# Casting, summing and testing the adjacency in half-row pieces during the graph convolutions of a four-layer graph network

## The chip, the cores and the metric

The kernel runs on one core of one Trainium2 chip. The metric is the device time of one execution in microseconds (us). A core has five engines that run side by side and meet at semaphores: TensorE (PE), VectorE (DVE), ScalarE (ACT), GpSimd (POOL) and SyncE (SP), which here only issues DMAs. Each engine runs its own list of instructions in order.

## What is computed

Sixteen graphs of N = 1024 nodes with D = 128 features; `adj` is a matrix of zeros and ones, 1024 x 1024 fp32 for each graph. Four residual layers follow each other, each on a layer norm with ReLU of x:

```python
def reference(x, adj, nodemask, ...):
    h = relu(layernorm(x)); x = x + gnn(h, adj, nodemask)     # dilate adj, three SAGE convolutions with batch norm, then Wl
    h = relu(layernorm(x)); x = x + attention(h, adj)         # softmax(q k' * scale + log(max(adj, 1e-8))), 4 heads
    h = relu(layernorm(x)); x = x + gat(h, adj)               # softmax over leaky_relu(s_i + s_j) where adj > 0
    h = relu(layernorm(x)); x = x + gcn(h, adj)               # D^-1/2 (adj + 1) D^-1/2 h W' + b, D from the row sums of adj + 1
    return x
```

The dilation drops neighbours row by row, and only the first layer uses its result. The other three layers use the whole `adj`. The batch norm of a convolution takes its mean and variance over all graphs, so each convolution layer ends before the next begins.

## The kernel before

The kernel has three stages, one after the other: `dilate_plain` (to about 690 us), `convolutions_plain` (to about 1606 us) and `attentions_plain` (to the end), and a short `verdict`. The fast path assumes, among other things, that `adj` holds only zeros and ones, is symmetric and has no empty row. Tests of this write into the tile `trouble` and the row sums into `deg`; `verdict` reads both at the end, and a general path runs if they speak against it.

**Dilation** leaves the thinned matrices of all graphs in a DRAM tensor `kept` as fp8 and reciprocal row sums in `rdeg`.

**Convolutions.** `neighbours(b, h)` (from line 1020) loads the thinned matrix of graph b (tile `C`, 1 MB, two buffers) and the reciprocal degrees broadcast to all partitions (`rdb`, 512 KB, two buffers), both on SP's queue. PE transposes h (L1029), ACT copies it out (L1030); a `Splitter` makes three bf16 parts of h on ACT and DVE (L676 to L679); PE multiplies them with C (L1040, 48 matmuls of 512 columns for a graph), and DVE scales the sums by `rdb` (L1042). A first loop over the graphs normalises x (loaded by POOL's queue, two buffers) and calls `neighbours`. Then three layers loop over the graphs: PE makes the output o (L1087 to L1094), ACT squares it (L1099), DVE sums the squares (L1100), POOL takes the power of -1/2 (`rsqrt`, L1045), ACT applies scale and ReLU (L1106), and in the first two layers `neighbours` follows. ACT's queue stores the result in `spill` (L1116). PSUM holds the outputs of two graphs, two neighbour sums and two turns. In this stage the framework orders the instructions of each engine when the program is built, by program order as priority and by its own estimate of when each is ready; the chip then keeps that order.

**Attention.** Seven generators (`matrices`, `before`, `attend`, `values`, `positive`, `gat`, `gcn`) each walk through the graphs. Each step says, with `yield`, which engine it needs next, for how long and from when; `in_order` (a planner that runs when the program is built) takes the step that can start first, on a tie one that is not for PE, and then the generator that lags most, and so fixes the order of each engine by hand. SP's DMAs stand in the order in which the generators emit them.

- `matrices` (L1301 to L1333) admits graph b once attention is done for the graphs up to b - 2 and the last layer up to b - 4 (`done["attend"] < b - 1`, `done["gcn"] < b - 3`). For each of eight row blocks it loads 128 x 1024 of `adj` in fp32 (L1309, 512 KB, two buffers `a`); ACT casts it to fp8 into the tile `A` with a ReLU and sums the rows (L1310); DVE tests for values other than zero and one (L1314); PE subtracts the turned blocks from the blocks below the diagonal (L1321, L1323) and ACT sums the absolute differences (L1327), which is the test of symmetry. `dinv` is made from `deg` (L1330, L1332). `A` has four buffers.
- `before` loads x and the three spilled convolution outputs (`h_a`, `hT_a`) on SP's queue, applies the layer's last product (L1354, L1357), the norm (L1274), turns it (L1283) and makes q, k and v (L1375, L1295).
- `attend` writes 16 A into PSUM (ACT, L1408), adds q k' (PE, L1413) and takes exponentials (ACT, L1421); `values` multiplies them with v and with ones (PE, L1444) and divides (DVE, L1450, L1452).
- `positive`, `gat` and `gcn` are the other two layers: masks (DVE, L1495), products with them (PE, L1555, L1570, L1624) and their sums (L1558, L1573), on splits into bf16 parts (L1541 to L1547, L1607 to L1613).

Of the kernel before, what the change touches and what calls it, by code (L numbers as in the profile page):

```python
# [6 lines left out]
F32 = mybir.dt.float32  # L7
# [5 lines left out]
ALU = mybir.AluOpType  # L13
# [948 lines left out]
def convolutions_plain(tc, x, ident, ap, xp, h0, minus_half, kept, rdeg, spill, final, Wr, Wx, bias, gamma, beta, Wl, bl):  # L962
    nc = tc.nc
    with ExitStack() as ctx:
# [3 lines left out]
        w2 = ctx.enter_context(tc.tile_pool(name="c_work", bufs=2))  # L968
        pso = ctx.enter_context(tc.tile_pool(name="c_out", bufs=4, space=PSUM))
# [76 lines left out]

        for b in range(B):
# [27 lines left out]
        wr_s, wx_s, constant = wr[0], wx[0], row_parts(b6[0], "const0")  # L1075
        for l in range(3):
            stats = kp.tile([P, 2 * B, 6], F32, name="stats")
            for b in range(B):
                if l:
                    rd6 = xp.tile([6, N], F32, name="xt")  # L1080
                    nc.sync.dma_start(rd6, rdeg[b][None, :].to_broadcast([6, N]))
                    has = w2.tile([6, N], BF16, name="has")
# [20 lines left out]
                rsqrt(nrm[:, 1, :], nrm[:, 0, :])  # L1103
                h = w2.tile([P, NB, D], F32, name="h")
# [3 lines left out]
                if l < 2:  # L1108
                    neighbours(b, h)
                else:  # L1110
# [38 lines left out]
        nc.vector.tensor_copy(final[3][0:3], row_parts(last, "const3")[0:3])  # L1149

# [55 lines left out]
def attentions_plain(tc, x, spill, final, ready_weights, adj, deg, trouble, eye, out, scores, bound, reach):  # L1206
    nc = tc.nc
    with ExitStack() as ctx:
# [7 lines left out]
        lp = ctx.enter_context(tc.tile_pool(name="f_load", bufs=2))  # L1216
# [28 lines left out]
        nc.vector.memset(trouble, 0.0)  # L1245
# [54 lines left out]
        def matrices():  # L1300

            for b in range(B):
                while done["gcn"] < b - 3 or done["attend"] < b - 1:
                    yield
                m = adp.tile([P, NB, N], F8, name="A")
                for i in range(NB):
                    t = yield "ACT", 1.3, 0.0, 0
                    a = lp.tile([P, N], F32, name="a")
                    nc.sync.dma_start(a, adj[b, i * P:(i + 1) * P, :])  # L1309
                    nc.scalar.activation(m[:, i, :], a, AF.Relu, accum_out=deg[:, b, i:i + 1], saturate=False)  # L1310
                    yield "DVE", 1.4, 0.0, 0
                    junk = lp.tile([P, N], F8, name="junk", bufs=1)

                    nc.vector.scalar_tensor_tensor(junk, a, 0.0, a, op0=ALU.is_gt, op1=ALU.not_equal,  # L1314
                                                   accum_out=trouble[:, b, i, 0:1], saturate=False)
                    for hf in range(2):
                        w = min(HN, (i - 4 * hf) * P)
                        if w > 0:
# [8 lines left out]
                            nc.scalar.activation(junk[:, :w], ps[:, :w], AF.Abs, accum_out=trouble[:, b, i, 1 + hf:2 + hf])  # L1327
# [412 lines left out]
def whole(tc, x, adj, nodemask, chunk_mats, chunk_mask, eye, sel, p, out):  # L1740
    nc = tc.nc
    with tc.tile_pool(name="dram", bufs=1, space=DRAM) as dp, tc.tile_pool(name="keep", bufs=1) as kp:
# [19 lines left out]
        with tc.tile_pool(name="final", bufs=1) as fp:  # L1762
            final = [fp.tile([P, D], F32, name=f"final{i}") for i in range(3)] + [fp.tile([3, D], BF16, name="final_row")]
            with tc.tile_pool(name="early", bufs=1) as yp, tc.tile_pool(name="c_adj", bufs=2) as ap, \
                    tc.tile_pool(name="c_x", bufs=2) as xp:
                ident = yp.tile([P, P], F32, name="ident")
                nc.sync.dma_start(ident, eye)
                minus_half = yp.tile([P, NB], F32, name="minus_half")
# [4 lines left out]
                convolutions_plain(tc, x, ident, ap, xp, h0, minus_half, kept, rdeg, spill, final, *layer0)  # L1773
            attentions_plain(tc, x, spill, final, ready_weights, adj, deg, trouble, eye, out, scores, bound, reach)
# [45 lines left out]
```

## Time and profile before

| | |
|---|---|
| median of 3 runs | 4039.99 us (4030.87 to 4042.07) |
| the profiled execution | 4039.04 us, span of its trace 4037.3 us |
| mean granted PE clock | 0.926 of full speed |
| PE busy | 3474.4 us (86%), 26756 matmuls |
| DVE busy | 2527.9 us (63%) |
| ACT busy | 2401.7 us (59%) |
| POOL busy | 794.7 us (20%) |
| read from and written to DRAM | 287.98 MB and 51.19 MB |

Busy time is summed over the span, so it mixes stages with different limits; the stages have to be looked at one by one. Instructions that only issue a DMA are not counted as busy, though they take time on their queue (SP, ACT or POOL). A line such as "PE x L1 <- ACT y L2: 10, 5, 3" in the table of waits means that PE's instructions of line 1 came late by 10 us in total, 5 times, at most 3 us, and that an instruction of line 2 on ACT ended the wait.

### The profile page before, as it was taken

To read this page: it belongs to the slowest core of one execution; us is meant where nothing else is said; L and a number is where in the kernel's file an instruction comes from. 1 tells how busy PE (TensorE), PEld (TensorE's weight loads), DVE (VectorE), ACT (ScalarE), POOL (GpSimd) and SP (SyncE) were. 2 spreads that over 40 slices of the span, in tenths; PEclk is the share of its full clock that TensorE was granted. 3 is DMA by queue.
4 is the path that set the end of the run, shared out by engine and by line. 5 is a ranking of instruction groups with operands and counts; after the bars stand their busy time and mean duration, and the time that the engine had idled before them with its cause. 6 is when DMAs were issued, how large, how long until landed. Compare 5 with 4: busy or idle time off the path is not lost.

```text
span 4037.3 us, 65855 instructions
## 1 busy us (share of the span) xinstructions
PE 3474.4 (86%) x26756; PEld 1998.6 (50%) x26756; DVE 2527.9 (63%) x4782; ACT 2401.7 (59%) x3961; POOL 794.7 (20%) x680
## 2 busy tenths in 40 slices
PE   4888887999999987778989988998898989989775
PEld 2556565445555566324444444444454444454333
DVE  4988774543344343328776876776777686777656
ACT  3778764543333334676667776767666767766540
POOL 7545521210000011101111112112111101211110
PEclk9999887999999998799999998999998999999887
DMA  9632223443333312411221221122122022111000
GB/s 106 40 21 16 14 97 116 165 159 126 125 111 121 108 68 85 142 37 53 74 79 43 64 79 60 51 74 74 43 69 80 26 74 79 58 59 48 27 17 17
DMA packets 182500, 293.21 MB, mean 73 GB/s; under 512 B 77468, under 2 KB 124456, under 8 KB 173992
## 3 DMA queue, kind: packets, MB, share of 16 engines
q1 hardware_dynamic: 91944, 221.69, 16.8%
q0 software_dynamic: 79728, 24.66, 7.5%
q10 hardware_dynamic: 10512, 42.54, 2.6%
q8 instruction: 212, 3.47, 0.4%
q14 instruction: 104, 0.85, 0.1%
HBM read 287.98 MB, written 51.19 MB: 84 GB/s over the span
## 4 chain that ended last, share of the span: by engine, by line
PE 58%; DVE 15%; ACT 7%; DMA 3%; issue 2%; POOL 2%; ACTq 0%; SPq 0%; POOLq 0%; DVEq 0%
PE g L1040 12%; PE acc L1444 9%; PE sum L1570 9%; PE t L1413 5%; PE sum L1624 4%; PE sum L1555 4%; DVE pm L1495 3%; PE o L1093 2%; PE sum L1357 2%; PE o L1094 2%; PE sum L1375 1%; ACT e L1421 1%; DVE rden L1450 1%; PE t L1029 1%; PE sum L1295 1%
## 5 line engine op out<-in xcount | busy, mean ns | idle before, releaser
L1421 ACT ACTIVATE e<-t 128x1024 f32<-128x1024 f32 x512 | 508.2, 1023 | 489.3 <-PE t L1413 472.9
L1495 DVE SCALAR_TENSOR_TENSOR pm<-dst,minus,A 128x1024 fp8e4<-128x1024 f32 x512 | 676.2, 1350 | 7.9 <-DMA dst<-scores 7.9
L1040 PE MATMUL g<-C,parts 128*128 128x512 fp8e4 x2304 | 521.3, 381 | 15.4 <-DVE aggT L1042 9.2
L1408 ACT ACTIVATE t<-A 128x2048 f32<-128x2048 fp8e4 x256 | 482.3, 1884 | 3.9 <-ACT dst L1475 0.3
L1570 PEld LDWEIGHTS <-pm 128*128 128x128 fp8e4 x4096 | 347.0, 98 | 187.1 <-issue 165.3
L1570 PE MATMUL sum<-parts,pm 128*128 128x198 bf16 x4096 | 400.3, 251 | 26.0 <-DVE pm L1495 16.3
L1444 PE MATMUL acc<-e,va 128*32 128x512 f32 x2048 | 330.5, 616 | 41.3 <-ACT e L1421 38.4
L1040 PEld LDWEIGHTS <-parts 128*128 128x128 bf16 x2304 | 223.1, 98 | 262.7 <-ACT parts L678 5.7
L1413 PE MATMUL t<-qT,kT 32*128 32x512 f32 x2048 | 307.7, 672 | 31.7 <-ACT t L1408 31.3
L1444 PE MATMUL acc<-e,ones_hd 128*32 128x512 f32 x2048 | 319.7, 601 | 0.0
L1573 DVE TENSOR_REDUCE pos<-sum 128x132 f32<-128x396 f32 x256 | 145.0, 566 | 204.0 <-PE sum L1570 203.4
L1555 PE MATMUL sum<-parts,A 128*128 128x396 bf16 x1024 | 210.8, 351 | 44.2 <-DVE parts L1547 23.9
L1042 DVE TENSOR_TENSOR aggT<-g,rdb 128x512 f32<-128x512 f32 x96 | 66.2, 690 | 269.2 <-PE g L1040 269.1
L1045 POOL TENSOR_TENSOR nrm<-nrm,minus_half 128x8 f32<-128x8 f32 x48 | 79.6, 1662 | 639.8 <-DVE nrm L1102 639.8
L1624 PE MATMUL sum<-A,gparts 128*128 128x512 fp8e4 x768 | 178.0, 385 | 24.9 <-ACT gparts L1607 17.6
L835 DVE TENSOR_TENSOR r<-ya,both 128x512 bf16<-128x512 f16 x184 | 140.2, 776 | 92.7 <-ACT ya L832 91.9
L1099 ACT ACTIVATE sq<-o 128x512 f32<-128x512 f32 x96 | 55.8, 599 | 226.1 <-PE o L1094 224.3
L1267 POOL TENSOR_TENSOR ln_st<-ln_st,minus_half 128x8 f32<-128x8 f32 x48 | 86.1, 1794 | 511.8 <-DVE ln_st L1265 377.1
L882 DVE SCALAR_TENSOR_TENSOR rows<-y,thirty,rows 128x1024 fp8e4<-128x1024 f16 x128 | 169.9, 1335 | 25.4 <-ACT y L874 24.6
L1555 PEld LDWEIGHTS <-A 128*128 128x128 fp8e4 x1024 | 94.5, 99 | 182.0 <-issue 104.1
L1106 ACT ACTIVATE h<-o,nrm 128x128 f32<-128x128 f32 x384 | 105.7, 384 | 116.9 <-POOL nrm L1045 113.7
L885 POOL TENSOR_TENSOR own<-rows,lower 128x256 bf16<-128x256 fp8e4 x128 | 109.5, 866 | 330.6 <-DVE rows L882 197.2
(287 smaller groups left out, 6937.7 us busy)
## 6 DMA issues: line engine op xcount, KB each, us to landing
a<-in_adj_dram SPq DMA_DIRECT2D x128, 512.0 KB
C<-kept SPq DMA_DIRECT2D x48, 1024.0 KB
dst<-scores SPq DMA_DIRECT2D x64, 512.0 KB
rdb<-rdeg SPq DMA_DIRECT2D x48, 512.0 KB
spill<-hT ACTq DMA_DIRECT2D x48, 512.0 KB
kept<-rows ACTq DMA_DIRECT2D x16, 1024.0 KB
h_a<-spill SPq DMA_DIRECT2D x64, 256.0 KB
hT_a<-spill SPq DMA_DIRECT2D x16, 512.0 KB
```

Source lines behind the costliest of these rows:

```text
L835: nc.vector.tensor_tensor(r, ya, both[:, 1, :, None].to_broadcast([P, G, P]), op=ALU.is_equal)
L882: nc.vector.scalar_tensor_tensor(row, y16, hh[:, g:g + 1], row, op0=ALU.not_equal, op1=ALU.mult, saturate=False)
L1040: nc.tensor.matmul(ps, parts[:, k, j, :], C[:, j, cols], start=j == 0 and k == 0, stop=j == NB - 1 and k == 2)
L1408: nc.scalar.activation(s, A[b][:, k, None, cols].to_broadcast([P, H, HN]), AF.Copy, scale=16.0)
L1413: nc.tensor.matmul(s[:, hd], kT[r, k * P:(k + 1) * P], qT[r, cols], start=False, stop=True, skip_group_check=True)
L1421: nc.scalar.activation(es[:, hd:hd + 2], s[:, hd:hd + 2], AF.Exp, scale=SIGMA)
L1444: nc.tensor.matmul(ps[r], ones if one else va[:, k, r], es[:, hd], start=k == 0, stop=k == NB - 1)
L1495: nc.vector.scalar_tensor_tensor(pm[:, i, :], dst[hd], minus[:, i, hd:hd + 1], A[b][:, i, :], op0=ALU.is_ge, op1=ALU.mult, saturate=False)
L1555: nc.tensor.matmul(ps[:, :3 * H * W], A[b][:, i, j * P:(j + 1) * P], parts4[:, i, :, :, W:], start=i == 0, stop=i == NB - 1)
L1570: nc.tensor.matmul(ps[:, jj * 6 * W:(jj + 1) * 6 * W], pm[:, i, (j + jj) * P:(j + jj + 1) * P], flat(parts4[:, i, hd]), start=i == 0, stop ...
L1573: nc.vector.reduce_sum(pos[:, j:j + 2, hd, :], ps[:, :12 * W].rearrange("p (j s w) -> p j w s", j=2, s=3), axis=AX.X)
L1624: nc.tensor.matmul(ps, parts[:, k, m, :], A[b][:, m, cols], start=m == 0 and k == 0, stop=False)
```

## The change

The cast to fp8 with its row sums and the test for zeros and ones leave `matrices` and go into `convolutions_plain`, as a function `look(n)` that works on the next n half row blocks (128 x 512; 256 of them in all). For each it loads the piece on SP's queue (256 KB, two buffers `a`), casts it on ACT into an fp8 piece (two buffers `m`), tests it on DVE, and stores the piece from ACT's queue in a new DRAM tensor `matrices` (64 KB, rows of 512 bytes). `look(4)` stands after each of the 16 `neighbours` calls of the first loop; in the layers 0 and 1 `look(3)` stands between the power and h, and `look(2)` after `neighbours`; in the last layer `look(2)` stands between the power and h. The two halves of each row sum are added once at the end of the stage.

`matrices` in the attention stage now loads the ready 1 MB of a graph with one DMA when the graph is admitted, and goes on to the symmetry test at once; it asks for no ACT or DVE step for cast and test any more, and the planner sees no need of the load. To make room, `rdb` and `has` have one buffer instead of two, and the attention stage's loading pool one instead of two. `trouble` gets a fourth column, and is zeroed by POOL at the beginning instead of by DVE in the attention stage.

```diff
@@ convolutions_plain
+        lp = ctx.enter_context(tc.tile_pool(name="c_load", bufs=2))
@@ neighbours
-            rdb = w2.tile([P, N], F32, name="rdb")
+            rdb = w2.tile([P, N], F32, name="rdb", bufs=1)
@@
+        halves = cp.tile([P, B, NB, 2], F32, name="halves")
+        parts_of = [(b, i, hf) for b in range(B) for i in range(NB) for hf in range(2)]
+
+        def look(n):
+
+            for b, i, hf in [parts_of.pop(0) for _ in range(n)]:
+                cols = slice(hf * HN, (hf + 1) * HN)
+                a = lp.tile([P, HN], F32, name="a")
+                nc.sync.dma_start(a, adj[b, i * P:(i + 1) * P, cols])
+                m = lp.tile([P, HN], F8, name="m")
+                nc.scalar.activation(m, a, AF.Relu, accum_out=halves[:, b, i, hf:hf + 1], saturate=False)
+                junk = lp.tile([P, HN], F8, name="junk", bufs=1)
+                nc.vector.scalar_tensor_tensor(junk, a, 0.0, a, op0=ALU.is_gt, op1=ALU.not_equal,
+                                               accum_out=trouble[:, b, i, 2 + hf:3 + hf], saturate=False)
+                nc.scalar.dma_start(matrices[b, :, i, cols].bitcast(F32), m.bitcast(F32))
@@ first loop over the graphs
             neighbours(b, h)
+            look(4)
@@ layers
-                    has = w2.tile([6, N], BF16, name="has")
+                    has = w2.tile([6, N], BF16, name="has", bufs=1)
@@
                 rsqrt(nrm[:, 1, :], nrm[:, 0, :])
+
+                look(3 if l < 2 else 2)
                 h = w2.tile([P, NB, D], F32, name="h")
@@
                 if l < 2:
                     neighbours(b, h)
+                    look(2)
@@ end of convolutions_plain
+        nc.vector.tensor_tensor(deg, halves[:, :, :, 0], halves[:, :, :, 1], op=ALU.add)
@@ attentions_plain
-        lp = ctx.enter_context(tc.tile_pool(name="f_load", bufs=2))
+        lp = ctx.enter_context(tc.tile_pool(name="f_load", bufs=1))
@@
-        nc.vector.memset(trouble, 0.0)
@@ matrices
                 m = adp.tile([P, NB, N], F8, name="A")
+                nc.sync.dma_start(m, made[b])
                 for i in range(NB):
-                    t = yield "ACT", 1.3, 0.0, 0
-                    a = lp.tile([P, N], F32, name="a")
-                    nc.sync.dma_start(a, adj[b, i * P:(i + 1) * P, :])
-                    nc.scalar.activation(m[:, i, :], a, AF.Relu, accum_out=deg[:, b, i:i + 1], saturate=False)
-                    yield "DVE", 1.4, 0.0, 0
-                    junk = lp.tile([P, N], F8, name="junk", bufs=1)
-
-                    nc.vector.scalar_tensor_tensor(junk, a, 0.0, a, op0=ALU.is_gt, op1=ALU.not_equal,
-                                                   accum_out=trouble[:, b, i, 0:1], saturate=False)
+                    t = 0.0
@@ whole
+        matrices = dp.tile([B, P, NB, N], F8, name="matrices")
-        trouble = kp.tile([P, B, NB, 3], F32, name="trouble")
+        trouble = kp.tile([P, B, NB, 4], F32, name="trouble")
@@
                 nc.sync.dma_start(ident, eye)
+                nc.gpsimd.memset(trouble, 0.0)
```

More of the change, by code (lines that the diff above doesn't have):

```diff
@@ L959, in norm_terms, with convolutions_plain @@
     nc.vector.tensor_scalar(st[:, 2], st[:, 2], 1.0 / D, LN_EPS, op0=ALU.mult, op1=ALU.add)
-def convolutions_plain(tc, x, ident, ap, xp, h0, minus_half, kept, rdeg, spill, final, Wr, Wx, bias, gamma, beta, Wl, bl):
+def convolutions_plain(tc, x, adj, matrices, deg, trouble, ident, ap, xp, h0, minus_half, kept, rdeg, spill, final, Wr, Wx, bias, gamma, beta, Wl, bl):
     nc = tc.nc
@@ L1149, in convolutions_plain @@
         nc.vector.tensor_copy(final[3][0:3], row_parts(last, "const3")[0:3])
+        assert not parts_of
+        nc.vector.tensor_tensor(deg, halves[:, :, :, 0], halves[:, :, :, 1], op=ALU.add)
 LOG_EPS = 18.420680743952367
@@ L1203, in attention_weights, with attentions_plain @@
         nc.sync.dma_start(into, t)
-def attentions_plain(tc, x, spill, final, ready_weights, adj, deg, trouble, eye, out, scores, bound, reach):
+def attentions_plain(tc, x, spill, final, ready_weights, made, deg, trouble, eye, out, scores, bound, reach):
     nc = tc.nc
@@ L1326, in matrices @@
                             junk = lp.tile([P, HN], BF16, name="junk2", bufs=1)
-                            nc.scalar.activation(junk[:, :w], ps[:, :w], AF.Abs, accum_out=trouble[:, b, i, 1 + hf:2 + hf])
+                            nc.scalar.activation(junk[:, :w], ps[:, :w], AF.Abs, accum_out=trouble[:, b, i, hf:hf + 1])
                 t = yield "DVE", 0.2, 0.0, 0
@@ L1772, in whole @@
                 dilate_plain(tc, adj, eye, kept, rdeg, unsettled, norm_first(tc, x, yp, h0, minus_half))
-                convolutions_plain(tc, x, ident, ap, xp, h0, minus_half, kept, rdeg, spill, final, *layer0)
-            attentions_plain(tc, x, spill, final, ready_weights, adj, deg, trouble, eye, out, scores, bound, reach)
+                convolutions_plain(tc, x, adj, matrices, deg, trouble, ident, ap, xp, h0, minus_half, kept, rdeg, spill, final, *layer0)
+            attentions_plain(tc, x, spill, final, ready_weights, matrices, deg, trouble, eye, out, scores, bound, reach)
         verdict(tc, nodemask, unsettled, trouble, deg, bound, reach, word)
```

## The prediction, on record before the change was run

> **What bounds the kernel now.** I read the page first (TensorE, PE, is busy 86% of the span), then the busy time of each engine by stage. Columns: stretch, its length, then PE, weight loads, DVE, ACT and POOL busy (instructions), PE clock, DMA share, GB/s.
> ```profile
> 694.00:890.00 196.00, 185.56 (x900) 91.94 (x901) 103.45 (x345) 101.49 (x229) 39.55 (x30) 0.96 0.48 164
> 890.00:1180.00 290.00, 278.15 (x1509) 169.63 (x1507) 109.66 (x200) 102.27 (x253) 26.76 (x17) 0.96 0.34 123
> 1180.00:1470.00 290.00, 274.93 (x1539) 167.54 (x1539) 118.49 (x212) 100.69 (x246) 25.11 (x16) 0.96 0.30 107
> 1470.00:1606.00 136.00, 111.80 (x765) 90.54 (x764) 53.53 (x94) 69.31 (x191) 27.27 (x17) 0.89 0.16 65
> 1606.00:1660.00 54.00, 30.82 (x148) 22.43 (x148) 24.03 (x65) 27.00 (x65) 7.81 (x4) 0.66 0.68 217
> ...
> 1800.00:3740.00 1940.00, 1737.26 (x13105) 923.50 (x13105) 1400.24 (x2026) 1333.82 (x1814) 308.53 (x162) 0.95 0.20 63
> ```
> The first four rows are the convolutions (first neighbour sums, layers 0, 1, 2): PE is nearly full, ACT and DVE are a third to half busy. In the attention stage ACT and DVE are at 69% and 72% and PE still idles 203 us of 1940. PE bounds both stages; what can be won is idle PE time, and only the attention stage has much. Whom PE waits for there, from 1640 us on (total, times, longest):
> ```profile
> PE acc L1444 <- ACT e L1421: 38.4, 36, 4.4
> PE sum L1295 <- DVE oT L1452: 31.5, 8, 9.1
> PE t L1413 <- ACT t L1408: 31.3, 20, 4.0
> PE sum L1357 <- DMA h_a<-spill: 25.3, 13, 6.1
> PE sum L1283 <- ACT h L1274: 24.0, 2, 17.2
> ...
> PE sum L1321 <- ACT A L1310: 17.3, 6, 6.2
> ```
> The waits are spread over ACT and DVE; L1310 (the cast) is named itself for little. SyncE's own waits show more of the moved work:
> ```profile
> SPq L1309 <- DVE junk L1314: 885.9, 116, 65.8
> ```
> SyncE's queue stands 886 us at the adjacency loads (two buffers, freed by the test L1314). What is behind them goes late. One instance, at 2901 us, in SyncE's and PE's order of time:
> ```profile
> 2901.30 0.33 SPq L1309 DMA_DIRECT2D a<-in_adj_dram  x1
> 2901.68 0.91 SPq L1348 DMA_DIRECT2D h_a<-spill  x2
> ```
> ```profile
> 2906.32 1.22 PE L1357 MATMUL sum<-final,h_a 128*128 128x128 f32 x3 [6.15 <-DMA h_a<-spill]
> ```
> The h_a loads went out the moment `a` got its buffer, and PE stood 6.15 us. The moved operations:
> ```profile
> L1314 DVE SCALAR_TENSOR_TENSOR junk<-a 128x1024 fp8e4<-128x1024 f32 x128 | 157.9, 1233 | 23.8 <-DMA a<-in_adj_dram 23.5
> L1310 ACT ACTIVATE A<-a 128x1024 fp8e4<-128x1024 f32 x128 | 135.3, 1058 | 31.4 <-DMA a<-in_adj_dram 31.4
> ```
>
> **What the Trainium skill says.** "VectorE: DVE Perf Modes", section "The TRN2 errata": VectorE and ScalarE pay a fixed cost per instruction, so many small tiles pay it many times; an fp32 tensor_tensor add takes (N+151)/0.96 ns. For N=1024 that is 1224, and L1314 took 1233: agreed. "ScalarE: Activation LUTs", section "What ACT_TABLE_LOAD costs": 186 ns + 0.833 N with immediate operands, 1039 for N=1024; L1310 took 1058. "DMA: Bandwidth & Descriptors", section "Anatomy of one DMA": some 2 us fixed beside the bytes (fitted for GpSimd's path), and a semaphore wait happens on the issuing sequencer ahead of dispatch, so it holds that queue. The 886 us agree with the second; for the first, the two h_a loads above, 512 KB behind 512 KB of `a`, took 4.6 us from issue to PE's start, so the fixed cost is of that size.
>
> **The change part by part. Removed from the attention stage.** ACT: 128 casts. With the accumulator read, one follows the other after 1.05 us (1617.91, 1618.96), so 134 us. DVE: 128 tests, 1.27 us apart (1617.69, 1618.96), 162 us. That is about a tenth of each engine's work there. SyncE: 128 loads of 512 KB with their buffer waits; in their place 16 loads of 1 MB whose buffers are free long before (the last reader of graph b-4 ends some 80 us before graph b is admitted). What this gives PE:
> - Start, 1606 to 1660: the first attend step comes at 1660, after 14 casts that share ACT with the first graph's norm, qT, kT and va; PE idles 23 us of 54. Cast and test waits go, but x, spill and 1 MB of A still have to land, and the chain of norm, transposes, qT, kT and va stays: 10 us of it.
> - h_a late behind `a`: 25.3 us after 1640 (5.6 before, in the start above). The serial queue behind `a` goes; I take 25.
> - L1321 waiting for the cast: 17.3, of which 13.6 after 1800: 14.
> - 3741 to 3758, PE idle 17.2 us: attention of the last graph starts only at 3762, since its matrix was complete at 3737, 130 us after it was admitted (3607), two casts at a time between other work. A ready matrix lets attention 15 start earlier: 17.
> - The rest: PE's gaps from 1800 to 3800 add up to 222 us; less 22 (h_a there), 14 and 17, about 169: waits on ACT and DVE queues, which have a tenth less in them. Laying the gaps over the ACT and DVE timelines, the cast runs inside 20 us of them and the test inside 24, partly the same. I take a fifth, 34.
> - New: the first check of a graph now waits for a 1 MB DMA that is emitted at admission. If SyncE issues it just then, PE waits 5 to 8 us; SyncE mostly runs ahead, so -10 over 14 graphs (0 to -60).
> Sum: 10+25+14+17+34-10 = **90 us gained** (50 to 140).
>
> **Added to the convolutions.** 256 half pieces. ACT: 1.05 less 512 x 0.833 ns = 0.62 us each; its DMA issue adds 0.33 us (as the spill stores, ACT queue at 1565.54). 256 x 0.95 = 243 us. DVE: 1.27 less 512/0.96 ns = 0.74 us, 189 us. Halving thus adds 25 us of ACT and 27 of DVE, and 84 of issue, all on engines with room. By stage (64, 80, 80, 32 pieces) ACT goes to (101+61)/196 = 83% with issue, (102+76)/290 = 61%, 61%, (69+30)/136 = 73%; DVE to 77%, 58%, 61%, 57%. PE stays the fullest everywhere, so the cost is only in order and latency:
> - First stage: two graphs take 23.3 us of PE (770.86 to 790.71 without a gap) and ACT has about 11 us idle in them, waiting for `parts` buffers; eight pieces need 7.7. Tight: 1 us per graph, 15 (0 to 60).
> - Layers 0, 1: ACT's gap for the power on POOL is 2.77 us (1209.68 to 1212.44), three pieces 2.9. At one place per two graphs PE has nothing else and already waits 1.52 us for L1106; a piece ahead of h adds about 1 us there: 16 (0 to 45).
> - Layer 2: 2.33 us of such wait per two graphs, two pieces: 1.5 x 8 = 12 (0 to 25).
> - rdb with one buffer: its load can start only after the preceding aggT. Already 40 of 48 loads waited for an aggT (24.6 us). It lands some 5 us later, while PE needs the freed sum bank only after another 5 us half, plus transposes: hidden; if traffic doubles the landing, 1 to 3 us for each of 16 graphs. Inside the first item. `has` with one buffer is read and freed within a layer's matmuls: nothing.
> - Queues: 256 loads on SyncE (0.33 us each) stand among C and rdb; C of b+2 may go out when g of b ends and has 11 us; 1 MB and two pieces of 256 KB are hidden at the 300 GB/s of the h_a case. First-stage traffic rises from 164 GB/s by 1.25 MB per 12 us to about 270. The ACT stores delay spill stores, which nobody awaits. POOL's zeroing of `trouble` instead of DVE's: under 1 us ahead of the first loads. 16 sums of the two halves are one small DVE instruction at the end: 0.3.
> Sum: 15+16+12+1 = 44, say **45 us lost** (15 to 130).
>
> Net -45 on the profiled execution's 4039 us (span 4037.3 and 1.7 around it), which lies 1 us under the median of 4040: **3994 us**.
>
> **The rivals.**
> *The convolutions swallow the pieces* (gain 110, cost 15): greedy filling of idle ACT time, as the 37% of ACT suggests. 4039-95 = 3944. Against it: PE's 1.5 and 2.3 us gaps show ACT is on the path once per pair.
> *A wash*: attention keeps its idle PE for other reasons (its waits are spread over ten releasers; the planned order also changes) and gains 45, the convolutions cost 45: 4039.
> *The pieces pace the convolutions* (slower). Place: ACT in the first stage and layers. Two `a` buffers and two `m` buffers, so a piece takes (landing + 0.74)/2. At the landing of 4.6 us that is 2.7 us, and 64 pieces need 171 of 196 us. From a landing of 5.4 us on (3.06 us a piece) the first stage is paced by them, and ACT, in order, stands at a late piece with parts and h behind it, for which PE waits. At 6.5 us: 3.6 x 64 = 232, +36; layers 0 and 1 reach 3.6 x 80 = 288 of 290, and half a microsecond of standing at each of 160 pieces is 80; layer 2 15. Cost 131 against a gain of 80: 4090. For it: 270 GB/s in the first stage. Against it: the DMA engines carried 217 GB/s at a share of 0.68, so 270 is about 0.85, high but not full.
>
> **How the numbers follow.** Forecast 0.50 (its own range 3960 to 4025), swallowed 0.15, wash 0.11, paced 0.24. About 0.3% (12 us) is what a measurement of this kernel can tell from no change. Faster: 0.50+0.15 = 0.65; same 0.11; slower 0.24. Range 3930 to 4075: the low end takes in the swallowed case and the full attention gain with a small cost, the high end reaches into the paced case and leaves out its far half and the lowest tail.
>
> **What would show it.** Right: the attention stage (1606 to the end) shorter by about 90 us, SyncE's 886 us gone, PE's waits for h_a under 5 us, none of 17 us ahead of attention 15; the convolutions (694 to 1606) longer by about 45, with PE's waits on L1106 grown. Paced: ACT and DVE waiting tens of us for the half-piece loads, and PE for parts. Wrong altogether: PE waits in the attention stage unchanged, or large new ones of L1321 on the A load.

## The result, and the profile after

The changed kernel takes **4069.12 us** (median of 7 runs, 4056.91 to 4079.53) against 4040.77 us (7 runs of the kernel before beside it). The ratio is **1.0071, 95% interval 1.0052 to 1.0091**: slower by 0.7%, where 3994 us was forecast. The profiled execution after took 4056.91 us (span 4054.6), the quickest of its seven, so the two traces differ by 18 us where the medians differ by 28.

The stages below begin and end at the first neighbour sum, the first spilled result of layers 0, 1 and 2, the first matmul of the attention stage, and the end. In us:

| stage | before | after | difference | forecast |
|---|---|---|---|---|
| first neighbour sums | 195.0 | 240.3 | +45 | +15 |
| layer 0 | 292.3 | 338.8 | +47 | +16 for both |
| layer 1 | 297.5 | 345.3 | +48 | |
| layer 2 | 130.7 | 130.4 | 0 | +12 |
| convolutions | 915.5 | 1054.8 | **+139** | +45 |
| attention | 2427.6 | 2306.2 | **-121** | -90 |

The busy times by stretch of the kernel after, in the columns that the prediction explains: the four stages of the convolutions, and the whole attention stage.
```profile
693.60:933.90 240.30, 198.95 (x910) 102.46 (x909) 144.67 (x485) 149.27 (x363) 39.91 (x30) 0.89 0.68 226
933.90:1272.70 338.80, 290.02 (x1517) 175.85 (x1516) 174.03 (x399) 167.81 (x447) 26.74 (x17) 0.92 0.60 199
1272.70:1618.00 345.30, 296.37 (x1568) 176.78 (x1568) 178.04 (x398) 168.21 (x443) 26.74 (x17) 0.89 0.55 178
1618.00:1748.40 130.40, 104.88 (x722) 84.44 (x721) 54.51 (x106) 65.31 (x180) 25.56 (x16) 0.88 0.18 72
...
1748.40:4054.60 2306.20, 2040.98 (x15316) 1070.73 (x15316) 1477.21 (x2157) 1433.62 (x1872) 357.83 (x192) 0.96 0.12 41
```
The same stretches of the kernel before:
```profile
694.20:889.20 195.00, 184.71 (x897) 91.55 (x898) 102.45 (x342) 100.49 (x227) 39.55 (x30) 0.96 0.47 164
889.20:1181.50 292.30, 280.45 (x1525) 171.41 (x1524) 111.74 (x205) 103.71 (x256) 26.76 (x17) 0.96 0.34 123
1181.50:1479.00 297.50, 280.98 (x1576) 171.91 (x1576) 119.36 (x216) 103.96 (x257) 26.76 (x17) 0.96 0.29 104
1479.00:1609.70 130.70, 104.85 (x719) 84.89 (x719) 53.72 (x107) 65.40 (x180) 26.11 (x16) 0.88 0.18 72
...
1609.70:4037.30 2427.60, 2082.37 (x15316) 1100.13 (x15316) 1634.87 (x2413) 1565.45 (x2128) 365.82 (x192) 0.93 0.19 60
```
PE's idle time is length less busy. In attention it fell from 345 to 265 us, by 80; and the same 15316 matmuls took 2041 instead of 2082 us, 41 less, at a higher granted clock. In the convolutions the opposite happened: idle time rose from 65 to 165 us over the four stages, by 100, and the same 4717 matmuls took 890 instead of 851 us, 39 more, at a clock of 0.89 to 0.92 in the first three stages instead of 0.96. So both stages moved the way that was forecast, and the convolutions paid more than attention got.

Below, a *piece* is one half row block, and a *ring* is the set of buffers that a tile takes in turn. Line numbers differ between the kernels: L1030, L1041, L1043 and L1128 of after are L1029, L1040, L1042 and L1106 of before; L1058, L1060, L1062 and L1064 are a piece's load, cast, test and store. Who made PE, ACT, DVE and SyncE's queue wait in the convolutions after (690 to 1745 us; total, times, longest):
```profile
PE t L1030 <- ACT h L1128: 58.6, 13, 8.1
PE g L1041 <- DVE aggT L1043: 56.8, 22, 6.1
...
ACT m L1060 <- DMA matrices<-m: 140.1, 78, 8.2
ACT m L1060 <- DMA a<-in_adj_dram: 126.4, 47, 7.7
...
DVE junk L1062 <- DMA a<-in_adj_dram: 228.9, 115, 5.4
...
SPq L1058 <- DVE junk L1062: 354.7, 178, 9.4
...
SPq L1058 <- ACT m L1060: 144.6, 101, 7.2
```
The first two lines before, in the same order (690 to 1606 us):
```profile
PE t L1029 <- ACT h L1106: 18.2, 12, 1.5
PE g L1040 <- DVE aggT L1042: 9.2, 3, 4.1
```
PE's waits in these two lines went from 27 to 115 us, which is most of the 100 us of new idle time. ACT and DVE are not too busy (62% and 60% of the first stage): they stand. ACT stands 140 us until the store of an older piece frees an `m`, and 126 us until a piece has landed; DVE stands 229 us for pieces. SyncE asks for a piece only when the test (355 us) or the cast (145 us) has freed its buffer. The cast itself, on the page (busy time, mean ns, then idle time ahead of it and its main cause), is as estimated:
```profile
L1060 ACT ACTIVATE m<-a 128x512 fp8e4<-128x512 f32 x256 | 161.6, 634 | 275.2 <-DMA matrices<-m 140.1
```
The test took 687 ns; the Trainium skill, "VectorE: DVE Perf Modes", section "The TRN2 errata", gives (N+151)/0.96 ns for an fp32 tensor_tensor add, which is 691 for N = 512. The work of a piece was forecast well; the waiting ahead of the pieces was not. How it reaches PE is seen in layer 0, from the after kernel's order of time (start, us, engine, operation, wait):
```profile
1115.20 0.69 DVE L1062 SCALAR_TENSOR_TENSOR junk<-a 128x512 fp8e4<-128x512 f32 x1 [2.88 <-DMA a<-in_adj_dram]
...
1116.04 0.69 DVE L1062 SCALAR_TENSOR_TENSOR junk<-a 128x512 fp8e4<-128x512 f32 x1
...
1116.65 0.69 DVE L1043 TENSOR_TENSOR aggT<-g,rdb 128x512 f32<-128x512 f32 x1
...
1117.39 0.38 PE L1041 MATMUL g<-C,parts 128*128 128x512 fp8e4 x1 [2.77 <-DVE aggT L1043]
```
```profile
1128.50 0.63 ACT L1060 ACTIVATE m<-a 128x512 fp8e4<-128x512 f32 x1 [8.20 <-DMA matrices<-m]
...
1136.04 0.63 ACT L1060 ACTIVATE m<-a 128x512 fp8e4<-128x512 f32 x1 [1.52 <-DMA matrices<-m]
...
1136.67 0.58 ACT L1119 ACTIVATE sq<-o 128x512 f32<-128x512 f32 x1
...
1141.02 0.48 PE L1030 MATMUL t<-ident,h 128*128 128x128 f32 x1 [5.12 <-ACT h L1128]
```
The sums g for the aggT of the first fence were complete at 1113.3, but DVE stood at a piece that landed at 1115.20, then tested another, and aggT came at 1116.65: PE lost 2.77 us. Then ACT stood 8.2 us at a store and, a piece at a time, until 1136.04; the square (L1119) stood behind, then the power and h, and PE lost 5.12 us.

In attention, PE's waits after (from 1745 us):
```profile
PE acc L1461 <- ACT e L1438: 33.3, 28, 6.8
...
PE sum L1319 <- DVE oT L1469: 5.8, 5, 2.0
...
PE sum L1338 <- DMA A<-matrices: 4.6, 1, 4.6
...
PE sum L1374 <- DMA h_a<-spill: 3.3, 6, 1.0
```
PE's waits in this stage before were 30.9 us for h_a, 31.5 for oT, 23.1 for the cast (now none; one wait of 4.6 us for a ready matrix stands in its place) and 23.9 for `parts` of L1547 (now none). Against that, waits for x of `before` (L1361, now L1378) grew from 12 to 29 us. SyncE's 886 us at the adjacency are gone.

### The profile page after: what moved, and what is told of

It reads as the page before. It is cut to its first block, busy times and chain, and to the rows that moved or that the text cites. A ratio compares the mean times of both kernels' runs of the same rounds, so it can differ in the third digit from the quotient of the medians.

```text
span 4054.6 us, 67420 instructions
## 1 busy us (share of the span) xinstructions
PE 3473.5 (86%) x26756; PEld 1990.3 (49%) x26756; DVE 2532.8 (62%) x5038; ACT 2446.1 (60%) x4217; POOL 788.0 (19%) x681
## 4 chain that ended last, share of the span: by engine, by line
PE 44%; DVE 17%; ACT 11%; DMA 10%; issue 2%; POOL 2%; ACTq 0%; POOLq 0%; SPq 0%; DVEq 0%
PE acc L1461 10%; PE sum L1587 8%; DMA a<-in_adj_dram 5%; PE t L1430 5%; DVE pm L1512 4%; PE sum L1572 3%; PE g L1041 3%; PE sum L1641 3%; DMA matrices<-m 2%; ACT e L1438 2%; DVE rden L1467 1%; POOL nrm L1046 1%; PE o L1113 1%; PE sum L1319 1%; PE sum L1392 1%
## 5 line engine op out<-in xcount | busy, mean ns | idle before, releaser
L1041 PE MATMUL g<-C,parts 128*128 128x512 fp8e4 x2304 | 539.1, 388 | 71.1 <-DVE aggT L1043 56.8
L1041 PEld LDWEIGHTS <-parts 128*128 128x128 bf16 x2304 | 226.7, 99 | 283.3 <-ACT parts L678 17.9
L1060 ACT ACTIVATE m<-a 128x512 fp8e4<-128x512 f32 x256 | 161.6, 634 | 275.2 <-DMA matrices<-m 140.1
L1062 DVE SCALAR_TENSOR_TENSOR junk<-a 128x512 fp8e4<-128x512 f32 x256 | 176.0, 687 | 233.2 <-DMA a<-in_adj_dram 228.9
L1430 PE MATMUL t<-qT,kT 32*128 32x512 f32 x2048 | 296.9, 650 | 27.5 <-ACT t L1425 27.3
L1596 POOL TENSOR_TENSOR pos<-pos,ex 128x1056 f32<-128x1056 f32 x16 | 45.8, 2860 | 860.6 <-DVE pos L1590 859.6
L1641 PE MATMUL sum<-A,gparts 128*128 128x512 fp8e4 x768 | 175.7, 382 | 23.7 <-ACT gparts L1624 17.7
L1113 PE MATMUL o<-wr,aggT 128*128 128x128 f32 x768 | 177.4, 317 | 0.0
```

The source lines that it names most:

```text
L1041: nc.tensor.matmul(ps, parts[:, k, j, :], C[:, j, cols], start=j == 0 and k == 0, stop=j == NB - 1 and k == 2)
L1113: nc.tensor.matmul(o, aggT[b][:, rows], wr_s, start=False, stop=False)
L1430: nc.tensor.matmul(s[:, hd], kT[r, k * P:(k + 1) * P], qT[r, cols], start=False, stop=True, skip_group_check=True)
L1641: nc.tensor.matmul(ps, parts[:, k, m, :], A[b][:, m, cols], start=m == 0 and k == 0, stop=False)
```

## The experiments

The theory after the result, **late pieces**: engines that keep their order stand at pieces whose load or store hasn't ended, since with two buffers each is asked for so late; aggT and h stand behind. Rivals: the buffer taken from `rdb`; the work of 256 casts and tests; the traffic of 64 MB in and 16 MB out. Times by stage are of one profiled execution each, and all but e9 are single executions; e6 and e9 are one kernel, with 1001 and 1009 us in the convolutions, so differences under some 10 us are not read, and those of 15 to 25 us are weak. In e1 to e4, e17 and e18 nothing is stored, so attention loads its matrices with one casting DMA each, on GpSimd's queue; their device times don't compare with the others.

| kernel | first | layer 0 | layer 1 | layer 2 | convolutions | attention | device |
|---|---|---|---|---|---|---|---|
| e1 no pieces | 194 | 289 | 297 | 131 | 911 | 2410 | 4016.14 |
| e2 loads only | 212 | 322 | 297 | 131 | 962 | 2412 | 4067.12 |
| e3 work only | 233 | 282 | 297 | 135 | 947 | 2407 | 4050.05 |
| e4 no store | 255 | 328 | 322 | 134 | 1038 | 2408 | 4145.67 |
| e5 loads on POOL's queue | 267 | 369 | 373 | 131 | 1140 | 2317 | 4150.68 |
| e6 four buffers each | 242 | 325 | 304 | 130 | 1001 | 2311 | 4001.58 |
| e7 two `rdb` | 247 | 341 | 338 | 130 | 1057 | 2311 | 4063.99 |
| e8 e5 with e7 and four `m` | 266 | 375 | 366 | 133 | 1139 | 2314 | 4146.40 |
| e9 as e6, 6 runs | 248 | 325 | 307 | 130 | 1009 | 2314 | 4012.13 |
| e10 four `a` | 248 | 366 | 334 | 130 | 1078 | 2313 | 4081.06 |
| e11 four `m` | 242 | 343 | 338 | 130 | 1054 | 2318 | 4066.15 |
| e12 even | 239 | 323 | 310 | 130 | 1002 | 2314 | 4007.79 |
| e13 ahead, two | 244 | 339 | 349 | 130 | 1062 | 2310 | 4062.05 |
| e14 ahead, four | 233 | 334 | 303 | 130 | 1000 | 2312 | 4011.52 |
| e15 gain alone | 195 | 292 | 296 | 132 | 915 | 2313 | 3983.41 |
| e16 e14 without tests | 243 | 304 | 307 | 130 | 984 | 2314 | 3988.68 |
| e17 loads only, five | 214 | 294 | 298 | 133 | 939 | 2409 | 4043.72 |
| e18 a quarter of e17 | 200 | 290 | 298 | 133 | 921 | 2406 | 4020.54 |

### e1 to e4: parts alone

All four take the store away and load `adj` in the attention stage; e1 takes the other three instructions of `look` too, e2 the cast and the test, e3 the load (cast and test work on one tile, loaded once), e4 nothing more.

```diff
-                nc.sync.dma_start(a, adj[b, i * P:(i + 1) * P, cols])
-                nc.scalar.activation(m, a, AF.Relu, accum_out=halves[:, b, i, hf:hf + 1], saturate=False)
-                nc.vector.scalar_tensor_tensor(junk, a, 0.0, a, op0=ALU.is_gt, op1=ALU.not_equal,
-                                               accum_out=trouble[:, b, i, 2 + hf:3 + hf], saturate=False)
-                nc.scalar.dma_start(matrices[b, :, i, cols].bitcast(F32), m.bitcast(F32))
...
-                nc.sync.dma_start(m, made[b])
+                nc.gpsimd.dma_start(m, made[b].rearrange('(i p) c -> p i c', p=P))
```


> Leaves out the pieces in the convolutions: no load, cast, test or store of half rows; row sums are a constant 8 and the values are not tested, so the last layer's output is not the reference's. The attention stage casts each graph's matrix in its 4 MB load on GpSimd's queue instead. rdb and has keep one buffer as in the changed kernel. Convolution stage, from the first neighbour sum to the first instruction of attention: 912 us before, 1051 changed. Theory 'late pieces' (ACT and DVE, in order, stand at loads and stores of pieces that come late): 912 +- 10, since nothing is late. Rival 'single buffers' (rdb and has are what costs): 950 or more.

> As e1, but with the 256 loads of 256 KB on SyncE's queue, which no engine reads; no cast, test or store. Theory 'late pieces': the loads alone delay C and rdb a little, 912 to 940. Rival 'traffic' (the added bytes and queue entries delay C and rdb, whatever the engines do): 990 or more.

> As e1, but with 256 casts and 256 tests of half rows on one resident piece: no loads, no stores, so no DMA wait. Row sums and tests are those of one piece. Theory 'late pieces': the work itself fills idle time, 912 to 945. Rival 'work' (ACT and DVE are on the path in the pairs of graphs, and 159 + 189 us of work show there): 990 or more.

> The pieces as in the changed kernel, loads, casts and tests, but without the 256 stores of 64 KB from ACT's queue (attention casts in its own load as in e1). Theory 'late pieces': ACT's 140 us of waiting for stores are half of its waits, so 970 to 1010. If only late loads count: 1030 to 1051. If only the stores count: below 940.

With no pieces the convolutions take 911 us, as before the change (916): **one buffer of `rdb` and `has` costs nothing** by itself. Loads alone cost 51 us and fell between the two expectations, work alone 36 (2 us over its expectation). In e3, with no load to wait for, the framework brought 165 of the 256 pieces into the first stage, where 67 ran in the changed kernel, so the 36 are not quite the price of the same work in its place. All but the store cost 127: e4 missed the 970 to 1010 of the theory and fell where only late loads were said to count. The store adds 17 more in the changed kernel (144 in all). 127 is 40 more than 51 and 36: loads and work are dearer together than apart, as they are if engines stand at loads. In e2 no engine reads the pieces, and still DVE waits for `rdb`, which stands behind them in SyncE's list (DVE's and SyncE's waits in e2's convolutions; L1059 is its piece load):
```profile
DVE aggT L1043 <- DMA rdb<-rdeg: 155.4, 21, 13.4
```
```profile
SPq L1059 <- DMA a<-in_adj_dram: 381.1, 231, 7.1
```
In the changed kernel DVE waited only 7.0 us for `rdb`, so the 51 us of e2 are not simply a part of the 144. e1 shows also what the forecast's item of the first check that waits for its load costs when a matrix is late (PE's waits in e1's attention stage); of the 121 us some 18 are left then, 2410 against 2428:
```profile
PE sum L1331 <- DMA A<-in_adj_dram: 83.8, 6, 17.2
```

### e5 to e8: another queue, more buffers

The edits in order: e5; e6 (to make room, the tiles sq, left, part and row get one buffer); e7 (the same room, `a` and `m` as in the changed kernel). e8 has the edits of e5 and e7, and `m` with four buffers.

```diff
-                nc.sync.dma_start(a, adj[b, i * P:(i + 1) * P, cols])
+                nc.gpsimd.dma_start(a, adj[b, i * P:(i + 1) * P, cols])
...
-                a = lp.tile([P, HN], F32, name="a")
+                a = lp.tile([P, HN], F32, name="a", bufs=4)
-                m = lp.tile([P, HN], F8, name="m")
+                m = lp.tile([P, HN], F8, name="m", bufs=4)
...
-            rdb = w2.tile([P, N], F32, name="rdb", bufs=1)
+            rdb = w2.tile([P, N], F32, name="rdb", bufs=2)
```


> The changed kernel with the 256 piece loads issued by GpSimd instead of SyncE, so that they don't stand behind C (1 MB) and rdb (512 KB) on one queue. Convolution stage 1055 us changed, 911 without pieces. Theory 'late pieces, made late by the queue they share': 960 to 1000. Rival 'late whatever the queue' (the fixed part of a load and two buffers): 1035 to 1065. GpSimd's own work (0.9 us an issue, 230 us in all, in front of the powers) could make it worse: over 1070.

> The changed kernel with four buffers for the loaded pieces and four for the cast ones; to make room, sq, left, part and row have one buffer. Theory 'late pieces' (a load that is asked for two pieces ahead comes late): with four ahead ACT and DVE stand much less, 950 to 990. Rival 'work' and 'traffic' (which need no waiting for pieces): e3 and e2 cost 36 and 51 us by themselves, so nothing below 998, 1000 to 1055.

> The changed kernel with two buffers for rdb again (sq, left, part and row have one to make room). With no pieces one buffer cost nothing (e1: 911 against 916). Theory: under the traffic of the pieces the one buffer shows, as in e2, where DVE waited 155 us for rdb: 1010 to 1035. Rival: aggT is late because DVE stands at pieces, not for rdb (7 us of waits for rdb in the changed kernel): 1050 to 1060.

> The changed kernel with piece loads on GpSimd's queue, two rdb buffers and four cast-piece buffers. If the three causes add: 911 + 36 of work + some 20 = 950 to 980, and the whole kernel about 3960 to 3990. If work on ACT and DVE in front of the critical steps is what costs: 1000 to 1040.

e5 missed my theory and hit what was feared of GpSimd: 1140 us. Its own waits in e5's convolutions:
```profile
POOL a L1058 <- ACT m L1060: 246.6, 68, 10.8
POOL a L1058 <- DVE junk L1062: 236.4, 74, 7.3
```
The Trainium skill, "DMA: Bandwidth & Descriptors", section "Anatomy of one DMA", says that a semaphore wait happens on the issuing sequencer ahead of the dispatch, so a wait for a buffer holds the engine that issues the load; these 483 us agree. On SyncE, in e2, that delayed `rdb`; on POOL it delayed the power, and so h: PE waited 116 us for h, at most 18.0. e8 has the same fault, and missed both of its expectations. e7, at 1057, found no gain in a second `rdb` buffer (no run has its four single-buffered tiles alone). e6 took back **54 us** with nothing but buffers; but its 1001 us missed the theory's 950 to 990 and lie just where the rivals, work and traffic, were said to leave it. So late pieces are not the only cause, and a rest is open.

### e9 to e12: e6 timed, and its buffers apart

e9 is e6 again; e10 is e6 with two `m`, e11 with two `a`; e12 is e6 with this:

```diff
-            look(4)
+            look(2)
...
-                look(3 if l < 2 else 2)
+                look(3 if l < 2 else 4)
```


> The changed kernel with four buffers instead of two for the loaded piece and for the cast piece (four small tiles of the convolutions get one buffer to make room), the same kernel as e6, now timed. If the one look of e6 (4001.6 beside 4038.2) stands for it: 0.988 to 0.994 of the kernel before, a median of 3993 to 4015. If e6 was a lucky single time: within 0.3% of before, 4028 to 4052.

> Four buffers for the loaded piece alone, two for the cast piece. If the late loads are what holds ACT and DVE (e6 got its gain from them; e4 without stores gained only 17 us): the convolutions take 1000 to 1020 us, device 3998 to 4022. If ACT at a store that hasn't ended holds the loaded pieces in turn, so that both are needed: 1035 to 1057, device 4035 to 4060.

> Four buffers for the cast piece alone, two for the loaded piece. If the late loads are what counts: 1035 to 1057 us for the convolutions, ACT's waits for the stores (140 us in the changed kernel) gone and its waits for loads grown instead. If the stores are what counts: 1000 to 1020.

> As e9, with two pieces instead of four behind each graph of the first loop and four instead of two in each graph of the last layer (32, 80, 80 and 64 pieces as written). If the framework leaves the first stage fewer pieces (under 60 where e6 had 79): the first stage 215 to 228 us instead of 242, layers 0 and 1 about as in e6 (325, 304), the last layer 135 to 150, convolutions 985 to 1000, device 3985 to 4000. If the framework moves the pieces forward as far as buffers allow, whatever is written: as many pieces in the first stage as in e6 (75 or more), and 995 to 1010 as in e6.

e9: 4012.13 us against 4031.76, **ratio 0.9947, 95% interval 0.9931 to 0.9963**; a gain of 0.5%; the median lies where e6 let expect it, the ratio just above the 0.994 I allowed. In e9's convolutions ACT and DVE stand less, and PE waits 72 us for h and aggT where it waited 115:
```profile
PE t L1030 <- ACT h L1128: 38.0, 11, 7.1
PE g L1041 <- DVE aggT L1043: 33.5, 12, 7.4
...
ACT m L1060 <- DMA matrices<-m: 65.9, 46, 6.3
...
ACT m L1060 <- DMA a<-in_adj_dram: 43.5, 22, 6.4
...
DVE junk L1062 <- DMA a<-in_adj_dram: 116.3, 73, 5.5
```
e10 overturned my guess that loads alone count, and missed both of its expectations: with four `a` and two `m` it is 1078, no better than two and two (1055). ACT's stand at loads shrank to 12 us, and it stands at the stores instead (e10's convolutions):
```profile
ACT m L1060 <- DMA matrices<-m: 252.3, 127, 7.7
```
With four `m` and two `a` (e11) ACT stands at the loads:
```profile
ACT m L1060 <- DMA a<-in_adj_dram: 239.7, 124, 7.2
```
e11 takes 1054. ACT stands 264, 244 and 267 us in all in e10, e11 and the changed kernel, and 109 in e9: **both rings have to be deep**, since an engine that keeps its order stands at whichever is late. e12 shows why the last layer cost nothing: written as 32, 80, 80 and 64 pieces, they ran as 73, 123, 60 and 0. The framework brings pieces forward as far as buffers allow. (The changed kernel, written as 64, 80, 80, 32, ran as 67, 96, 93, 0.)

### e13 to e18: what is left

In e13 two loads are asked for ahead of the loops, and `look` asks for one more after each piece (first part); e14 does so with four, and with the buffers and the room of e6; e16 is e14 without the test. e15 has an empty `look` as e1, attention as in the changed kernel, and the second part ahead of the dilation. e17 is e2 with five buffers, e18 is e17 with the third part.

```diff
-                a = lp.tile([P, HN], F32, name="a")
-                nc.sync.dma_start(a, adj[b, i * P:(i + 1) * P, cols])
+                a = asked.pop(0)
...
                 nc.scalar.dma_start(matrices[b, :, i, cols].bitcast(F32), m.bitcast(F32))
+                ask()
...
+                full = yp.tile([P, N], F8, name="full")
+                nc.gpsimd.memset(full, 1.0)
+                for b in range(B):
+                    for i in range(NB):
+                        nc.sync.dma_start(matrices[b, :, i].bitcast(F32), full.bitcast(F32))
...
-                nc.sync.dma_start(a, adj[b, i * P:(i + 1) * P, cols])
+                nc.sync.dma_start(a[:, :P], adj[b, i * P:(i + 1) * P, hf * HN:hf * HN + P])
```


> The changed kernel, but each load is asked for in the program two pieces ahead of its use, directly after the cast, test and store of the piece that held its buffer; still two buffers. If the loads come late because the program asks for them late (they stand behind C, rdb and other work in SP's list): convolutions 1010 to 1035 us instead of 1055, device 4010 to 4035. If only the number of buffers holds them: 1045 to 1065.

> As e13, four pieces ahead, with four buffers for the loaded and four for the cast piece as in e9 (convolutions 1009 us, DVE waiting 116 us and ACT 44 us for loads). If the loads that are asked for late make up the rest: those waits under 60 us together, convolutions 960 to 985, device 3960 to 3985. If the buffers have already given all: 1000 to 1012, device 4000 to 4015.

> The attention stage of the changed kernel, the convolutions without any piece: nothing is loaded, cast, tested or stored there; 128 stores early in the dilation fill the ready matrices with ones, row sums are the constant 8. It leaves out the casts, row sums and tests, and attention runs on a matrix of ones. If the attention stage's gain stands by itself: attention 2300 to 2320 us as in the changed kernel (2306), convolutions 908 to 920, device 3905 to 3930. If part of the 121 us depended on when the pieces of the convolutions end: attention 2330 or more, device 3940 or more.

> As e14 without the tests for zeros and ones on DVE, which it leaves out; loads, casts and stores stay. If DVE standing at a test ahead of aggT is what is left of the cost: the waits of PE for aggT (33 us in e9) gone and the convolutions 25 to 45 us shorter than in e14. If ACT and the traffic are: within 12 us of e14.

> As e2, the loads alone, but with five buffers. It leaves out casts, tests, row sums and stores; the attention stage gets its matrices from a casting load. If e2's 51 us came from SP standing at a buffer whose load hasn't landed, with rdb behind it: SP's wait at the loads under 100 us instead of 381, convolutions 912 to 930. If the bytes themselves (the DMA engines' share of 0.77) delay C and rdb: 945 to 965.

> As e17 with a quarter of each load (128 columns of 512): the same 256 loads in SP's list, 16 MB instead of 64. If the bytes are the cost in e17: convolutions within 10 us of the stage without pieces, 908 to 922. If SP's list of 256 more loads is the cost whatever they carry: within 10 us of e17.

e13 (1062 against 1055) and e14 (1000 against 1001 and 1009) say that it matters little where the load stands in the program: **the buffers set when it is asked for**. e16: without tests 984, 16 us less than e14, under the 25 that I gave a DVE cause and over the 12 of its rival; DVE is a part only. e15: attention 2313 and convolutions 915, so the gain stands by itself, within 7 us. Its device time missed (3983 for 3905 to 3930), because the stores of ones held back the first loads (PE's waits in e15's first 690 us); the convolutions began 59 us later than in the kernel before, and 3983 less 59 is 3924:
```profile
PE turn L1208 <- DMA C<-in_L_gnn_W_dram: 72.5, 1, 72.5
```
e17: five buffers halve what loads alone cost, from 51 to 28 us. It lies between the two expectations, nearer to the queue: SyncE's queue still stands at its own loads, more than the 100 us I allowed.
```profile
SPq L1059 <- DMA a<-in_adj_dram: 153.4, 159, 6.5
```
e18: a quarter of the bytes leaves 10 of these 28, no more than the scatter, so a longer list by itself costs little. With the bytes SyncE's stand at its own loads fell too, to 63 us. So of the 51 us that loads alone cost, some 23 are too few buffers, and 18 are the bytes with the waiting that they bring.

## Why the prediction was wrong

**The convolution cost (45 us, range 15 to 130) failed**, at 139. The three estimates "first stage 15 (0 to 60)", "layers 0, 1: 16 (0 to 45)" and "layer 2: 12" were +45, +95 and 0. They counted the time that a piece *works* (0.62 us on ACT and 0.74 on DVE; the trace has 0.63 and 0.69, with 0.19 and 0.08 for reading the sums, partly at the same time) and asked whether it fits into idle time. For work alone the sum was near: 43 us in these three, 36 in e3, though in the three places it was 38, -7 and 4 (rounded) instead of 15, 16 and 12, so the agreement is partly luck. The step that failed is the item "Queues": it took the loads as hidden, said of the stores only that they delay others which nobody awaits, and so the sum has no term for engines that wait for a piece. It took 300 GB/s from the h_a case, whose 1 MB in 4.6 us is 226; nor do these 4.6 us, which hold a load's fixed cost and its bytes together, show the fixed cost that the prediction read from them. More than the rate, it missed that an engine *stands at a piece* that was asked for late: 267 us on ACT and 229 on DVE, with aggT, the square and h behind. With loads the work cost 127 us, with stores 144. Undone one by one: rings of four instead of two take back 46 to 54 us (e9, e6), leaving out the tests about 16 more (e16), and 73 over the stage without pieces are left. If the loads cost there what they cost alone with five buffers (28, e17), some 45 lie in casts, stores and their remaining waits; no run tells these apart.

**The rival "the pieces pace the convolutions"** (4090 us: cost 131, gain 80) was the nearest by size, but is only partly what happened. It had two buffers and engines kept in order right. But it named one threshold, a landing of 5.4 us, and the time from SyncE's issue of a piece to its last packet (each load matched with its packets in order) was 3.0 us in the median, 5.8 at the ninetieth percentile and 8.3 at most. Nor were the slow ones the main thing: 91 of DVE's 115 waits, 150 us of its 229, were for pieces that landed within 4 us of their issue; the 36 pieces over 5.4 us took 67. On ACT these shares are 54 and 65 us of 126. So most of DVE's standing is not a late landing but a late issue: SyncE asked for the piece only when its buffer came free. The rival did not price the stores: the ring of `m` stops ACT for 140 us, as much as the loads do. PE's waits for `parts`, its sign, stayed small: 14 us. Traffic was less than I feared: 226 GB/s at a share of 0.68 in the first stage, for 270 at 0.85.

**The attention gain (90 us, range 50 to 140)** was right in kind: 121, and PE's idle time alone 80. By its items (forecast, then measured over the whole stage): h_a 25, and 27.6 (30.9 to 3.3); L1321 14 less 10 for the load, and 18.5 (23.1 to 4.6); start 10, and 8 (the first attend step comes 42 us into the stage instead of 50; some of this is in the two items before). The 17 us ahead of the last graph's attention are gone, but a wait of 14.7 us for a layer norm stands in the tail at 3900 to 4054, so that PE's idle time in the last 400 us fell only from 102 to 89: 13. The fifth of the remaining gaps, 34, has no measured counterpart: oT gave 25.7 and `parts` 23.9, partly in that tail, while waits for x took back 17. The four items sum to at most 67 of the 80 us, so some 13 or more came from the rest.

**A second term was missing on both sides: how fast matmuls run after a pause.** 41 us in attention and 39 in the convolutions come from the same number of matmuls at another granted clock, and nearly cancel. With idle time alone the change would stand at +20 (100 less 80), and with the whole it stands at +18; so the term does not explain the sign. The idle time in the convolutions does: had it risen by the 45 forecast, the rest as measured would have been a gain of about 37.

That a single buffer for `rdb` and for `has` costs nothing, held (e1; e7 for `rdb`). That the planner sees no need of the load is harmless as long as the matrix is there (4.6 us after), and costs some 84 us of PE's waits when it isn't (e1).

## What to carry to other kernels

Work moved into idle time on an engine that keeps its order costs, beside the work, what the engine stands at it (here 36 us for work alone, 144 with loads and stores). Count, for every buffer ring that the work runs through (load and store), what frees a buffer, when the next transfer is therefore asked for and how long it takes from then, and name what is queued behind. Deepen all rings of the chain together; in e10 and e11 one alone only moved the wait. A load that waits for a buffer also holds what stands behind it on its queue (`rdb` on SyncE in e2, the power on GpSimd in e5); no run here had a queue with nothing urgent behind.

## What the runs showed of the hardware

**A pause of 2.77 us was followed by a stretch at a lower PE clock.** It is the pause that ended at 1117.39 in the layer 0 example. The same columns for the 3.9 us after it and for 9.8 us ahead of it:
```profile
1117.30:1121.20 3.90, 3.81 (x18) 2.82 (x18) 3.90 (x8) 2.90 (x7) 0.00 (x0) 0.67 0.96 334
...
1103.60:1113.40 9.80, 9.80 (x49) 4.64 (x49) 4.42 (x11) 5.17 (x17) 1.64 (x1) 1.00 0.71 236
```
Taken finer, the clock was 1.00 for 1.2 us after the pause, 0.51 for the next 3.4 (1118.6 to 1122.0), and 1.00 again; a pair of L1113's matmuls took 0.63 instead of 0.39 us. The Trainium skill, "TensorE: Matmul & The Clock Gate", section "What's actually happening", has the clock halved after an idle window of about 3.4 us and released after a busy one of that length. The half clock and the length of its stay agree with this trace; the pause was shorter than the page's window. Over the stages, the matmul time that the half clock cost, worked out from the clock record, is 41 us before and 81 after in the convolutions, and 111 and 66 in attention: the 39 us more and 41 less of matmul time above. They go with 100 us more and 80 us less of idle time.

**A casting load can make PE wait longer than the cast did.** The 4 MB loads of e1 on GpSimd's queue took 13.5 to 17.7 us from issue to landing, and PE waited 83.8 us for them in six waits, where it had waited 23.1 us for the cast before and 4.6 for ready 1 MB loads after. The whole stage was still 18 us shorter than before.

**The time from issue to landing of a 256 KB piece didn't shrink with more buffers** (median 3.6, ninetieth percentile 6.7 in e6 against 3.0 and 5.8): they only let it be asked for sooner.
